# Attention's first tiles, image 0's convolution and gates, and the gathering of results: four edits in a transformer kernel

## The chip, the cores and the metric

The kernel runs on one core of a Trainium2 chip, whose engines TensorE (PE), VectorE (DVE), ScalarE (ACT) and GpSimd (POOL) run their own instruction streams, while SyncE (SP), ACT and POOL issue transfers (DMA). The metric is the device time of one execution in microseconds, as the median of several runs. Everything is float32.

## The reference

The input x is 4 images of 384 channels and 32 x 32 pixels (1024 tokens each, 4096 in all).

```python
# layer 0
x = x + conv0(_ln_c(x))      # attention: 8 heads of 48, q k and v by one matrix of 384 x 1152
#   attn = q k^T + q table_k[idx] + (k table_q[idx])^T, softmax, out = attn v + (attn summed by idx) table_v, projection
#   idx: the clipped offset (dy, dx) of two pixels, 15 x 15 of them
t = t + ffn0(_ln_t(t))       # factored (Kronecker) weights, gelu
# layer 1
x = x + conv1(_ln_c(x))      # depthwise: 7x7 + 5x3 + 3x5 + (1x7, 7x1) + (1x5, 5x1) + bias
probs = softmax(_ln_t(t) @ gate_w + gate_b)   # 4 experts, the best 2, weights made to sum to 1
t = t + sum over the 2 experts of weight * (gelu(_ln_t(t) @ w1[e] + b1[e]) @ w2[e] + b2[e])
```

## The kernel before

The work is in three phases, one after the other.

`qkv_phase` (to 233 us) takes 8 tiles t of 512 tokens, two to an image. For each, PE makes six 128 x 512 blocks of q and k, DVE scales each into `qk_sb` (four buffers) and POOL's queue stores it to `qk_d` in DRAM (L168); the next tile's statistics follow; then PE makes v in four blocks of 128 tokens, which ACT scales into `va`, a tile that holds v of all heads and tokens. After every second tile `va`'s part of one image (2 MB) is stored to `v_d` on POOL's queue (L183). After tiles 2 to 5, POOL's queue also writes zeros over a quarter of `xs_d` (L191), in two writes of 3 MB each; `xs_d` will hold the rows of tokens sorted by expert.

`attention_phase` (233 to 1681 us) takes the heads in turn, some 176 us each. For a head, `load_tables` brings the table `tab` and the head's q or k (`kq`) in and `load_keys` the keys as the scores use them (`kk`); PE multiplies tables and q or k (`tabq_ps`, `tabk_ps`), DVE transposes 32-wide blocks (L306), ACT copies to `st`, and SP stores to `sd` in DRAM, from where the position terms come back in the order of the scores. Then for each of 32 rows of pixels: the bias is summed on POOL (L352), scores on PE, their sum and maximum on DVE (L380), exponentials on ACT (L390), transposes and products with v. The next head's loads and table products run in the shadow of the present head's; those of the first head have nothing to hide behind. Its loads stand on ACT's queue. The memory of this phase lies over that of the qkv phase, so that `kq`, `kk`, the memory of `arow` and that of `den` wait for the last read of `va`. Matmuls and loads of this phase are kept in the order in which they are written (`pin`); most others are ordered by a scheduler that estimates costs, so that the built order on an engine need not be that of the code.

`rest_phase` (from 1681 us) begins with `enter(0)`, that is `front(0)` (attention's projection, its residual, and the first feed-forward), and with `first()` (normalisation and convolution of image 0). The convolution's 49 taps are split by channel chunk k and rows: `convolve` runs on DVE, one multiply-add per tap and part (L996), and `taps_by_matmul` on PE, with a diagonal weight block per tap; sums of even and odd taps stand in two halves of two banks (`tap_ps`), are folded by a further matmul into a bank `taps_ps` (L1050), which is single, and DVE adds that to `xb` (L1053). Of image 0, DVE has chunk 0 and half of chunk 1, PE chunk 2 and the other half of chunk 1. `dispatch(0)` then makes the gates (`gates`: logits, token statistics, weights and mask) and sorts the tokens: positions, and 16 indirect writes (`scatter`). All that concerns images 1 to 3 is one generator, `others()`, called `todo`: `front`, normalisation, convolution on DVE, gates and scatter of each image, cut in steps. Two of its steps are run per step of `dispatch(0)`.

Then come 67 blocks of 128 sorted tokens (`blocks`), about 16 us each: POOL gathers a block's rows (`xg`) and, when the expert changes, weights (`w`), PE transposes the rows and makes both products (L1193, L1175), and steps of `todo` are mixed in while their estimated DVE time is behind that of PE. In the last group of blocks, after the sixth, `combine(range(B - 1))` is mixed in too, one step per half block: for every 256 tokens of images 0 to 2, four indirect gathers of expert outputs `y`, a weighted sum (ACT, then DVE at L1243), six transposes on PE (`out_ps`, L1221), an addition to the residual `xr` (a load from `x2_d`, one buffer), and the output store on SP's queue. `combine([3])` follows after the last block.

Of the kernel before, what the change touches and what calls it, by code (L numbers as in the profile page):

```python
# [11 lines left out]
F32 = mybir.dt.float32  # L12
AF = mybir.ActivationFunctionType
# [5 lines left out]
P = 128  # L19
# [16 lines left out]
VW = 64  # L36
# [84 lines left out]
def qkv_phase(tc, cst, x, w_qkv, qk_d, v_d, xs_d):  # L121
# [6 lines left out]
    with ExitStack() as es:  # L128
# [22 lines left out]
        for t in range(NT // TOK):  # L151
            b, n0 = divmod(t * TOK, N)
            xt = xts.pop(t)
            _, rstd = stats
            ps = to_partitions(nc, (work, psum, "st"), ident, one, rstd)
            scale = work.tile([P, TOK], F32, tag="scale", name="scale")
            nc.scalar.copy(scale, ps)
            if t + 1 < NT // TOK:
                load(t + 1)
            for m in range(2 * KC):  # L160
                ps = psmm.tile([P, TOK], F32, tag="mm", name="qk_ps")
                for k in range(KC):
                    nc.tensor.matmul(
                        ps, wq[:, k, m * P : (m + 1) * P], xt[:, k, :], start=(k == 0), stop=(k == KC - 1)
                    )
                sb = ev.tile([P, TOK], F32, tag="qk", name="qk_sb")
                nc.vector.tensor_tensor(sb, ps, scale, ALU.mult)
                nc.gpsimd.dma_start(qk_d[m * P : (m + 1) * P, t * TOK : (t + 1) * TOK], sb)  # L168
            if t + 1 < NT // TOK:
                stats = result(token_stats(nc, (work, psum, "st"), ident, xts[t + 1], cst["eps6"]))  # L170
            for j in range(TOK // P):
                ps = psmm.tile([P, TOK], F32, tag="mm", name="v_ps")
                for k in range(KC):
                    nc.tensor.matmul(
                        ps[:, :C], xt[:, k, j * P : (j + 1) * P], wq[:, k, 2 * C :], start=(k == 0), stop=(k == KC - 1)
                    )
                nc.scalar.activation(
                    va[:, :, t * (TOK // P) + j, :HD], ps[:, :C].rearrange("p (h d) -> p h d", d=HD),
                    AF.Copy, scale=rstd[:, j, :],
                )  # L180
            if n0 + TOK == N:
                w = NBLK * VW
                nc.gpsimd.dma_start(  # L183
                    v_d.rearrange("h p n -> p h n")[:, :, b * w : (b + 1) * w],
                    va[:, :, b * NBLK : (b + 1) * NBLK, :].rearrange("p h c d -> p h (c d)"),
                )
            if 2 <= t < 2 + NEXP:
                rows = xs_d[(t - 2) * CAP : (t - 1) * CAP].rearrange("(n p) c -> p n c", p=P)
                n = rows.shape[1] // 2
                for r in (rows[:, :n], rows[:, n:]):  # L190
                    nc.gpsimd.dma_start(r, bcast(zero, 1, r.shape[1]))  # L191


def attention_phase(tc, cst, tabs, tv, qk_d, v_d, ao_d, heads):

# [28 lines left out]
    with ExitStack() as es:  # L226
# [24 lines left out]
            den.append(d)  # L251


        kq = fixed.tile([64 + HD, NT], F32, name="kq")
        kk = fixed.tile([64 + HD, B, N // 2], F32, name="kk")
        tab = fixed.tile([64 + HD, SPAN, ZW], F32, name="tab")
        vb = fixed.tile([P, B, NBLK, VW], F32, name="vb")
        aT = fixed.tile([P, NBLK, YB, P], F32, name="aT")
        a1t = fixed.tile([P, 4, IMG, YT, B], F32, name="a1t")
        tvw = fixed.tile([P, 4, IMG, HD], F32, name="tvw")  # L260

        def load_tables(h):
            for lo, i, r0 in ((64, 0, h * HD), (0, 1, C + h * HD)):
                bulk(tab[lo : lo + HD], tabs[i, h])
                yield
                for b in range(B):
                    bulk(kq[lo : lo + HD, b * N : (b + 1) * N], qk_d[r0 : r0 + HD, b * N : (b + 1) * N])
                    yield
# [239 lines left out]
            sd = dram.tile([P, IMG, SPAN * IMG], F32, tag="sd", name="sd")  # L508
            return [{"h": h, "y": y, "sd": sd} for y in range(IMG)], prepare(h, sd)

        for _ in load_tables(heads[0]):
            pass
        load_keys(heads[0])
        blk, tables = new_head(heads[0])
# [323 lines left out]
def rest_phase(tc, cst, x, ao_d, ins, xs_d, y_d, x2_d, out):  # L838
# [9 lines left out]
    with ExitStack() as es:  # L848
# [167 lines left out]
        def taps_by_matmul(xb, parts):  # L1016
# [10 lines left out]

            half = small.tile([P, 64], F32, tag="half", name="half", bufs=1)
            nc.vector.tensor_tensor(half, ident[:, :64], ident[:, 64:], ALU.add)
            diag = {k: diagonals(k, w) for k, w in zip(dict.fromkeys(k for k, _ in parts), wts[1])}  # L1030
            yield
            for k, y0 in parts:
                sums = [ps_y.tile([P, TOK], F32, tag="y", name="tap_ps", bufs=2) for _ in range(2)]
                for t0 in range(0, 49, 2):
                    for t in range(t0, min(t0 + 2, 49)):
                        dy, dx = divmod(t, 7)
                        for h in range(2):
                            lo = 64 * h
                            nc.tensor.matmul(
                                sums[h][64 * (t % 2) : 64 * (t % 2) + 64].rearrange("p (y x) -> p y x", x=IMG),  # L1040
                                diag[k][lo : lo + 64, t, :],
                                img[lo : lo + 64, k, dy + y0 : dy + y0 + TOK // IMG, dx : dx + IMG],
                                start=(t < 2), stop=(t > 46),
                            )
                    yield
                po = ps_y.tile([P, TOK], F32, tag="t", name="taps_ps")
                for h in range(2):
                    e = hid.tile([P, TOK], F32, tag="hs", name="taps", bufs=HS)
                    nc.scalar.copy(e, sums[h])
                    nc.tensor.matmul(po[64 * h : 64 * h + 64], half, e, start=True, stop=True)  # L1050
                yield
                acc = xb[:, k, y0 * IMG : y0 * IMG + TOK]
                nc.vector.tensor_tensor(acc, acc, po, ALU.add)  # L1053
                yield

        def new(shape, name, dt=F32):
# [151 lines left out]
        def combine(bs):  # L1208
# [13 lines left out]
                    nc.vector.tensor_tensor(xr[:, c0:c1, :], xr[:, c0:c1, :], ps[:, : c1 - c0, :], ALU.add)  # L1222
                nc.sync.dma_start(out[b, :, n0 : n0 + w].rearrange("(k p) n -> p k n", p=P), xr)

            late = None
            for b, n0 in ((b, n0) for b in bs for n0 in range(0, N, w)):
                t0 = b * N + n0
                if n0 == 0 and not end:
                    result_rows(nc, small, images[b], pieces)
                    if b + 2 == B:  # L1230
                        result_rows(nc, small, images[b + 1], pieces)
                    yield 3.0, 0.0
                zs = []
                for j in range(2):
                    ys = []
                    for s in range(2):
                        y = new_row() if end else ld.tile([P, C], F32, tag=f"yt{s}", name=f"yt{s}")
                        index = images[b]["pos"][:, n0 // P + j, s : s + 1]
                        nc.gpsimd.indirect_dma_start(y, None, y_rows, bass.IndirectOffsetOnAxis(ap=index, axis=0))
                        ys.append(y)  # L1240
                    gate = images[b]["gate"][:, n0 // P + j, :]
                    nc.scalar.activation(ys[0], ys[0], AF.Copy, scale=gate[:, 0:1])
                    nc.vector.scalar_tensor_tensor(ys[0], ys[1], gate[:, 1:2], ys[0], ALU.mult, ALU.add)  # L1243
                    zs.append(ys[0])
                if end:
                    if late:
                        finish(*late)
                    xr = xbs[b][:, :, n0 : n0 + w]
                    late = (b, n0, xr, zs)
                    yield 0.0, 0.0  # L1250
                else:
                    xr = ld.tile([P, KC, w], F32, tag="xr", name="xr", bufs=1)
                    nc.sync.dma_start(xr, x2_d[:, t0 : t0 + w].rearrange("(k p) n -> p k n", p=P))
                    for _ in range(6):
                        yield 0.4, 0.1
                    finish(b, n0, xr, zs)
            if late:
                finish(*late)

        xbs = {}  # L1260

# [8 lines left out]
        def first():  # L1270


            taps = taps_by_matmul(xbs[0], [(2, 0), (2, IMG // 2), (1, IMG // 2)])
            next(taps)
            halves = []
            yield from normalise(xbs[0], halves)
            yield from image(halves)
            for _ in convolve(0, xbs[0], [(0, 0, IMG), (1, 0, IMG // 2)]):
                for _ in range(2):
                    next(taps, None)  # L1280
                yield
            for _ in taps:
                pass
            preload(wts[1])
# [40 lines left out]
        for i, _ in enumerate(first()):  # L1325
            if 6 <= i < 8:
                next(todo)
        for _ in dispatch(0):
            for _ in range(2):
                next(todo)  # L1330
        clock = [0.0, 0.0]

# [28 lines left out]
def metaformer_kernel(ctx: ExitStack, tc: tile.TileContext, ins, out):  # L1361
# [15 lines left out]
    x2_d = dram.tile([C, NT], F32, name="x2_d")  # L1377
    xs_d = dram.tile([NEXP * CAP, C], F32, name="xs_d")
    y_d = dram.tile([ALL * BLK, C], F32, name="y_d")
    qkv_phase(tc, cst, ins["x"], ins["w_qkv"], qk_d, v_d, xs_d)  # L1380
    attention_phase(tc, cst, ins["tabs"], ins["tv"], qk_d, v_d, ao_d, list(range(HEADS)))
    rest_phase(tc, cst, ins["x"], ao_d, ins, xs_d, y_d, x2_d, out)


# [66 lines left out]
```

## Time and profile before

| | us |
|---|---|
| median of 3 runs | 3321.61 (3317.27 to 3322.02) |
| the profiled execution | 3319.24 |
| its span | 3317.4 |
| PE busy | 2985.4 (90%) |
| DVE busy | 2012.0 (61%) |
| ACT busy | 1327.9 (40%) |
| POOL busy | 1149.2 (35%) |

All busy times are within the span; what is outside the span (1.8 us) is the start and end of the execution that no instruction covers. A profile row of a group gives line, engine, operation, output and input with their shapes, the number of instructions, busy time and the mean of one in ns. A row of waits gives the engine and what it was about to run, then the instruction or transfer that released it, total us, times and longest. In rows of stretches, the number in brackets counts instructions, and after the five engines come the granted PE clock (1.00 is full), the busy share of the DMA engines and GB/s. Lines are those of the kernel before.

### The profile page before, as it was taken

What the parts mean: (1) busy time and instruction counts of PE and PEld (TensorE: products, weight loads), DVE (VectorE), ACT (ScalarE), POOL (GpSimd) and SP (SyncE); (2) the same over time, 40 slices, a digit from 0 to 9 for tenths busy, and PEclk for the clock granted to TensorE, in tenths of its full rate; (3) what the DMA queues carried; (4) which work ended last, traced back from release to release, by engine and by line L of the source; (5) the groups of instructions that cost most, each with busy time, mean ns of one, the idle gap of its engine ahead of it and who ended that gap; (6) DMA issues with size and microseconds to landing.
All of it is one profiled execution on the core that took longest, in us unless ns stands there. A gap on an engine that the chain in (4) does not pass through costs nothing.

```text
span 3317.4 us, 63687 instructions
## 1 busy us (share of the span) xinstructions
PE 2985.4 (90%) x25391; PEld 2067.9 (62%) x25391; DVE 2012.0 (61%) x3618; ACT 1327.9 (40%) x2682; POOL 1149.2 (35%) x1096
## 2 busy tenths in 40 slices
PE   8988898989898989898879697999999999999897
PEld 4445666656675666666643354576677777777675
DVE  2226777867677777777748779999999520002101
ACT  1115555555555655565511131443342423333222
POOL 3113636363636364544520031123124231214312
PEclk9998999999999999999989888999999999999898
DMA  8637464555455554646240222271344044466652
GB/s 308 242 115 208 111 183 118 171 132 163 127 173 127 160 147 132 178 120 189 69 151 25 100 69 100 83 289 55 119 184 184 27 179 156 155 262 220 230 203 72
DMA packets 222136, 500.57 MB, mean 151 GB/s; under 512 B 92128, under 2 KB 144992, under 8 KB 214160
## 3 DMA queue, kind: packets, MB, share of 16 engines
q1 hardware_dynamic: 156080, 212.81, 21.0%
q0 software_dynamic: 43488, 228.24, 18.7%
q10 hardware_dynamic: 22272, 55.46, 6.8%
q8 instruction: 200, 3.28, 0.4%
q14 instruction: 96, 0.79, 0.1%
HBM read 543.58 MB, written 152.37 MB: 210 GB/s over the span
## 4 chain that ended last, share of the span: by engine, by line
PE 61%; DVE 12%; issue 9%; DMA 7%; ACT 6%; POOL 4%; SPq 1%; ACTq 0%; POOLq 0%; DVEq 0%
PE e_ps L1193 13%; PE y_ps L1175 13%; DVE xb L996 7%; PE av_ps L216 6%; PE tabq_ps L216 5%; PE t_ps L409 5%; PE sc_ps L216 4%; PE tv_ps L216 3%; ACT arow L390 2%; PE tabk_ps L216 2%; ACT aT L410 2%; PE a_ps L419 2%; DMA qs<-qk_d 2%; DVE oT L473 2%; POOL bias L352 1%
## 5 line engine op out<-in xcount | busy, mean ns | idle before, releaser
L352 POOL TENSOR_TENSOR bias<-b,s 128x416 f32<-128x416 f32 (+24 forms) x656 | 659.5, 1042 | 654.6 <-DMA s<-sd 474.3
L1193 PEld LDWEIGHTS e_ps<-xT,w 128*128 128x128 f32 x4824 | 660.0, 194 | 238.4 <-issue 17.0
L1193 PE MATMUL e_ps<-xT,w 128*128 128x128 f32 x4824 | 680.0, 279 | 23.4 <-DVE xb L909 9.2
L1175 PE MATMUL y_ps<-w,eh 128*128 128x384 f32 x1608 | 656.0, 493 | 8.7 <-DVE yo L1178 4.8
L996 DVE SCALAR_TENSOR_TENSOR xb<-img,c_w,xb 128x1024 f32<-128x1024 f32 (+1 forms) x539 | 630.2, 1227 | 0.0
L1196 ACT ACTIVATE eh<-e_ps,w 128x128 f32<-128x128 f32 x804 | 294.4, 368 | 765.0 <-PE e_ps L1193 750.7
L380 DVE CUSTOM_DVE_ANT_0 arow<-sc_ps,bias 128x1024 f32<-128x1024 f32 x256 | 312.6, 1221 | 192.3 <-POOL bias L352 80.3
L1165 POOL DMA_INDIRECT w<-in_w,row x134 | 163.9, 1223 | 747.6 <-PE y_ps L1175 232.3
L401 DVE TENSOR_REDUCE extra<-arow 128x32 f32<-128x32 f32 (+24 forms) x768 | 378.8, 551 | 28.3 <-ACT arow L390 28.0
L409 PEld LDWEIGHTS t_ps<-ident,arow 128*128 128x128 f32 x2048 | 227.6, 144 | 265.5 <-ACT arow L390 184.0
L410 ACT COPY aT<-t_ps 128x512 f32<-128x512 f32 x512 | 276.0, 589 | 266.0 <-PE t_ps L409 249.9
L390 ACT ACTIVATE arow<-arow,nm 128x1024 f32<-128x1024 f32 x256 | 297.1, 1161 | 177.9 <-DVE nm L380 166.8
L409 PE MATMUL t_ps<-ident,arow 128*128 128x128 f32 x2048 | 290.0, 286 | 77.4 <-ACT arow L390 74.5
L1178 DVE TENSOR_TENSOR yo<-y_ps,w 128x384 f32<-128x384 f32 x67 | 37.1, 553 | 496.0 <-PE y_ps L1175 496.0
L216 PE MATMUL sc_ps<-kk,qs 48*32 48x512 f32 x4096 | 295.8, 623 | 46.6 <-DVE nm L380 27.6
L1175 PEld LDWEIGHTS y_ps<-w,eh 128*128 128x128 f32 x1608 | 250.2, 194 | 22.2 <-ACT eh L1196 5.2
L306 DVE STREAM_TRANSPOSE b<-tabk_ps 128x480 f32<-128x480 f32 x256 | 219.7, 979 | 62.2 <-PE tabq_ps L216 36.8
L216 PEld LDWEIGHTS av_ps<-aT,vb 128*64 128x64 f32 x4096 | 223.0, 137 | 52.8 <-ACT aT L410 38.0
L216 PE MATMUL tabq_ps<-tab,kq 48*128 48x480 f32 x512 | 225.2, 587 | 19.9 <-DMA kq<-qk_d 19.9
L216 PE MATMUL av_ps<-aT,vb 128*64 128x128 f32 x4096 | 238.4, 275 | 0.3 <-ACT aT L410 0.3
L216 PE MATMUL tabk_ps<-tab,kq 48*128 48x480 f32 x512 | 225.4, 587 | 0.0
L216 PEld LDWEIGHTS tabq_ps<-tab,kq 48*128 48x128 f32 x512 | 147.6, 296 | 57.7 <-issue 26.5
(217 smaller groups left out, 3147.1 us busy)
## 6 DMA issues: line engine op xcount, KB each, us to landing
sd<-st SPq DMA_DIRECT2D x128, 480.0 KB, 2.5
s<-sd SPq DMA_DIRECT2D x512, 120.0 KB, 3.3
xs_d<-zero POOLq DMA_DIRECT2D x8, 3072.0 KB, 11.4
tvw<-in_tv ACTq DMA_DIRECT2D x120, 192.0 KB, 3.7
y_d<-yo SPq DMA_DIRECT2D x67, 192.0 KB, 2.0
qk_d<-qk_sb POOLq DMA_DIRECT2D x48, 256.0 KB, 3.4
qs<-qk_d SPq DMA_DIRECT2D x256, 48.0 KB, 2.9
kq<-qk_d ACTq DMA_DIRECT2D x64, 192.0 KB, 3.7
```

The source lines that it names most:

```text
L216: ins = nc.tensor.matmul(*args, **kw)
L306: turn = nc.vector.transpose(b2.rearrange("p e y x -> p x (e y)")[:, i + j], ps[:, j, : SPAN * IMG])
L352: nc.gpsimd.tensor_tensor(bias[:, y0:y1, :], bass.AP(b2.tensor, b2.offset + (e * IMG + y0) * IMG, [list(b2.ap[0]), [(step * IMG + 1) * IMG ...
L380: nc.vector.tensor_tensor_reduce(s["flat"], ps.rearrange("p h n -> p (h n)"), s["bias"].rearrange("p y x -> p (y x)"), -SCALE, BIG, ALU.ad ...
L390: nc.scalar.activation(s["flat"], s["flat"], AF.Exp, bias=s["nm"], scale=-1.0, accum_out=dn[:, y % YT : y % YT + 1])
L401: pin(nc.vector.tensor_reduce(ex[:, i, :], a[:, p0:p1, :].rearrange("p y x -> p x y"), AX.X, ALU.add))
L409: pin(nc.tensor.transpose(pt[:, j, :], s["flat"][:, k0 : k0 + P], ident))
L410: pin(nc.scalar.copy(aT[:, 4 * g : 4 * g + 4, s["y"] % YB, :], pt))
L996: nc.vector.scalar_tensor_tensor(acc[:, k, y0:y1], img[:, k, dy + y0 : dy + y1, dx : dx + IMG], w7[:, k, dy, dx : dx + 1], acc[:, k, y0:y1 ...
L1175: nc.tensor.matmul(py, hs, w[:, o : o + C], start=(ff == 0), stop=(ff == NF - 1))
L1193: nc.tensor.matmul(ph, w[:, o : o + P], xT[k][:, c, :], start=(c == 0), stop=(c == KC - 1))
L1196: nc.scalar.activation(hs, ph, AF.Gelu, bias=w[:, o : o + 1])
```

## The change

Four things change.

- `kq`, `kk` and `tab` come from a pool `held` that is opened before the qkv phase, so that they have memory of their own. The first head's tables are loaded on SP's queue instead of ACT's. v is stored to `v_d` after every tile (1 MB), and the zero writes are kept in program order, where the scheduler had placed them singly before.
- In image 0's convolution, DVE has chunk 0 and 4 rows of chunk 1; PE has chunk 2 in two parts of 16 rows and the other 28 rows of chunk 1 in two parts of 14. The steps of PE's taps are taken three instead of two per tap of DVE.
- `dispatch(0)` takes no step of `todo` in its first six steps, and three per step after that.
- In the combine, the gathers and the residual load of a chunk of 256 tokens are issued one chunk ahead; the rows stand in the 16 buffers named `rows`, the residual has two buffers; a chunk has ten steps instead of six. All images' result rows are made first. At the end all 16 gathers are issued ahead of the sums.

```diff
-            if n0 + TOK == N:
-                w = NBLK * VW
-                nc.gpsimd.dma_start(
-                    v_d.rearrange("h p n -> p h n")[:, :, b * w : (b + 1) * w],
-                    va[:, :, b * NBLK : (b + 1) * NBLK, :].rearrange("p h c d -> p h (c d)"),
-                )
+            w = NBLK // 2 * VW
+            nc.gpsimd.dma_start(
+                v_d.rearrange("h p n -> p h n")[:, :, t * w : (t + 1) * w],
+                va[:, :, t * NBLK // 2 : (t + 1) * NBLK // 2, :].rearrange("p h c d -> p h (c d)"),
+            )
...
-                    nc.gpsimd.dma_start(r, bcast(zero, 1, r.shape[1]))
+                    tc.keep_in_program_order(nc.gpsimd.dma_start(r, bcast(zero, 1, r.shape[1])))
...
-        kq = fixed.tile([64 + HD, NT], F32, name="kq")
-        kk = fixed.tile([64 + HD, B, N // 2], F32, name="kk")
-        tab = fixed.tile([64 + HD, SPAN, ZW], F32, name="tab")
+        kq, kk, tab = held
...
-        for _ in load_tables(heads[0]):
+        for _ in load_tables(heads[0], dma):
             pass
...
-            for k, y0 in parts:
+            for k, y0, ny in parts:
+                n = ny * IMG
...
-            late = None
-            for b, n0 in ((b, n0) for b in bs for n0 in range(0, N, w)):
-                ...
-                        y = new_row() if end else ld.tile([P, C], F32, tag=f"yt{s}", name=f"yt{s}")
-                ...
-                    xr = ld.tile([P, KC, w], F32, tag="xr", name="xr", bufs=1)
-                    nc.sync.dma_start(xr, x2_d[:, t0 : t0 + w].rearrange("(k p) n -> p k n", p=P))
-                    for _ in range(6):
-                        yield 0.4, 0.1
-                    finish(b, n0, xr, zs)
+            def results(b, n0):
+                zs = []
+                for j in range(2):
+                    ys = [new_row() for _ in range(2)]
+                    for i, y in enumerate(ys):
+                        index = images[b]["pos"][:, n0 // P + j, i : i + 1]
+                        nc.gpsimd.indirect_dma_start(y, None, y_rows, bass.IndirectOffsetOnAxis(ap=index, axis=0))
+                    zs.append(ys)
+                if end:
+                    return zs, xbs[b][:, :, n0 : n0 + w]
+                t0 = b * N + n0
+                xr = ld.tile([P, KC, w], F32, tag="xr", name="xr")
+                nc.sync.dma_start(xr, x2_d[:, t0 : t0 + w].rearrange("(k p) n -> p k n", p=P))
+                return zs, xr
+
+            def weigh(b, n0, zs):
+                ...
+            if not end:
+                for b in (*bs, B - 1):
+                    result_rows(nc, small, images[b], pieces)
+                    yield 3.0, 0.0
+            todo = [(b, n0) for b in bs for n0 in range(0, N, w)]
+            ahead = {}
+            for i, (b, n0) in enumerate(todo):
+                for more in todo[i : i + (len(todo) if end else 2)]:
+                    if more not in ahead:
+                        ahead[more] = results(*more)
+                zs, xr = ahead[b, n0]
+                for _ in range(0 if end else 5):
+                    yield 0.3, 0.0
+                zs = weigh(b, n0, zs)
+                for _ in range(0 if end else 5):
+                    yield 0.3, 0.1
+                finish(b, n0, xr, zs)
...
-            taps = taps_by_matmul(xbs[0], [(2, 0), (2, IMG // 2), (1, IMG // 2)])
+            half, own = IMG // 2, 4
+            rest = (IMG - own) // 2
+            taps = taps_by_matmul(
+                xbs[0], [(2, 0, half), (2, half, half), (1, own, rest), (1, own + rest, rest)]
+            )
...
-            for _ in convolve(0, xbs[0], [(0, 0, IMG), (1, 0, IMG // 2)]):
-                for _ in range(2):
+            for _ in convolve(0, xbs[0], [(0, 0, IMG), (1, 0, own)]):
+                for _ in range(3):
                     next(taps, None)
                 yield
...
-        for _ in dispatch(0):
-            for _ in range(2):
+        for i, _ in enumerate(dispatch(0)):
+            for _ in range(3 if i > 5 else 0):
                 next(todo)
...
+    with tc.tile_pool(name="held", bufs=1) as pool:
+        held = [
+            pool.tile([64 + HD, *n], F32, name=name)
+            for name, n in (("kq", [NT]), ("kk", [B, N // 2]), ("tab", [SPAN, ZW]))
+        ]
+        qkv_phase(tc, cst, ins["x"], ins["w_qkv"], qk_d, v_d, xs_d)
+        attention_phase(tc, cst, held, ins["tabs"], ins["tv"], qk_d, v_d, ao_d, list(range(HEADS)))
```

## The prediction

> **What bounds the kernel now.** I read the page first: shares of the engines, then the chain that ended last.
>
> ```profile
> span 3317.4 us, 63687 instructions
> ...
> PE 2985.4 (90%) x25391; PEld 2067.9 (62%) x25391; DVE 2012.0 (61%) x3618; ACT 1327.9 (40%) x2682; POOL 1149.2 (35%) x1096
> ...
> PE 61%; DVE 12%; issue 9%; DMA 7%; ACT 6%; POOL 4%; SPq 1%; ACTq 0%; POOLq 0%; DVEq 0%
> ```
>
> PE is the bound almost everywhere, so a gain can only come out of the 332 us in which it is idle, or out of work that it does at half clock. Where those are is read from busy times by stretch (start:end in us, length, busy us of each engine with its instruction count, granted PE clock, DMA share, GB/s). I cut the span where the stages that the change touches begin and end:
>
> ```profile
> 90.00:105.00 15.00, 10.44 (x34) 5.90 (x33) 4.56 (x12) 1.46 (x3) 2.28 (x3) 0.89 1.02 386
> 233.00:294.00 61.00, 36.73 (x160) 25.45 (x160) 27.33 (x35) 19.67 (x34) 7.85 (x10) 0.77 0.77 227
> 1778.00:1876.00 98.00, 75.61 (x605) 32.20 (x598) 93.06 (x102) 4.47 (x8) 0.00 (x0) 0.88 0.20 77
> 1876.00:1959.00 83.00, 71.90 (x266) 30.97 (x267) 47.51 (x170) 32.10 (x59) 24.94 (x23) 0.90 0.23 80
> 2600.00:2985.00 385.00, 380.13 (x2302) 298.89 (x2301) 42.67 (x238) 125.77 (x320) 85.27 (x85) 0.99 0.45 166
> 2985.00:3135.00 150.00, 127.50 (x750) 101.01 (x750) 30.26 (x55) 45.61 (x112) 65.31 (x67) 0.92 0.64 211
> ```
>
> Each is a place where PE is short of work or slow: 4.6 us idle with DMA saturated; 24 us at attention's start; 22 us in image 0's convolution, where DVE is full; 22.5 us in the combine against 5 in the 385 us before it. The chain over attention's start (start, length, what) and one step of it at 80 us:
>
> ```profile
> 80.14 16.01 DMA qk_d<-qk_sb
> ...
> 234.29 7.51 DMA v_d<-va
> 242.57 2.00 ACTq L224
> 246.01 6.39 DMA kq<-qk_d
> 252.86 5.94 PE tabq_ps L216 x7
> 262.77 0.39 PE tabq_ps L216
> 284.37 2.52 DMA sd<-st
> 291.80 1.88 POOL bias L352
> ```
>
> The last qkv matmul ends at 232.96; the 2 MB store of v must be read out of `va` before anything of attention may overwrite that memory; then the tables and q load; PE starts at 252.86, at half clock. Last, VectorE's forms in the convolution (mean ns of one), and what PE waited for there and in 2985 to 3135 (total, times, longest):
>
> ```profile
> L996 DVE SCALAR_TENSOR_TENSOR xb<-img,c_w,xb 128x1024 f32<-128x1024 f32 x49 | 62.4, 1274 | 0.0
> L996 DVE SCALAR_TENSOR_TENSOR xb<-img,c_w,xb 128x512 f32<-128x512 f32 x49 | 36.3, 740 | 0.0
> ```
> ```profile
> PE taps_ps L1050 <- DVE xb L1053: 18.8, 1, 18.8
> ```
> ```profile
> PE out_ps L1221 <- DVE yt L1243: 16.6, 5, 10.1
> PE xT_ps L1159 <- DMA xg<-xs_d,slot: 5.7, 2, 3.7
> ```
>
> **Attention's start.** `kq`, `kk` and `tab` no longer share addresses with `va`, and their first loads stand on SP's queue, in the built order among the qkv tiles; the last is issued with the last tile, about 4 us ahead of PE's end. So PE's first table product waits only for its own queue: from the end E of the qkv matmuls, about E+0.6, against 19.9 us before, and the clock doesn't fall. What still waits for the last v store (now one tile, 1 MB; the 2 MB took 7.51 us, so about 4 with issue and semaphore to E+6) are the memsets of `arow` and `den`, and behind `den` on DVE the 31 table transposes: 261.28 to 288.75 before, 25.9 us of work (0.81 us each), so E+6.5 to E+32.5. The last `st` copy stood 4.4 us ahead of their end, and the first bias on POOL 6.8 us behind that copy (store, reads, q loads): E+28 to E+31, bias at E+35 to E+38. Before it was 291.2 − 233.0 = 58.2. I take 37: **−21**, bounds −23 and −19. SP takes these ten loads and the first two of q; it had nothing but x tiles and weights there.
>
> **The qkv stage itself.** Before, one tile (t=2) took 31.8 us where the others take 25.36; its first evacuation waited for a `qk_d` store that took 16.01 us, queued on POOL behind a 3 MB zero write and the 2 MB v store. That loss, 6.5, can go. Against it: the eight zero writes, spread before over 15 to 106 us, are now two together behind the v store of t = 2 to 5. A tile then moves x 0.79, q and k 1.57, v 1.05, zeros 6.29 and about 0.39 MB of early q loads: 10.1 MB. If only POOL's queue counts (a zero write drains in 7.6 to 9 us, so 17 for a pair, 2.8 for v, 2 for the x tile it meets, and latencies: 25.7 us), a tile is 0.3 us over PE's 25.36: 1.4 in four. The Trainium skill (*DMA: Bandwidth & Descriptors*, "Issuing engines are not separate DMA queues") says that queues of all issuers end on the same 16 engines and interleave, so that moving loads to SP buys no bandwidth; with the 386 GB/s of the saturated row, 10.1 MB take 26.2 us: 0.8 a tile, 3.3 in four. The row at 1.02 DMA share agrees that the engines, not a queue, are full; I take 3.3. Net **−3**, bounds −6.5 and +6. PE's v part isn't behind the late evacuations (in the built order DVE's two last ones follow the next tile's statistics), which is why a late store costs no more than its own overrun.
>
> **Image 0's convolution.** DVE's second form shrinks from 512 to 128 elements. Start to start a pair takes 1.858 us (1.196 and 0.662), which gives 1.043 ns an element and 0.128 fixed: 0.26 us. 49 × (1.196 + 0.26) = 71.4 against 91.0: DVE's taps end at 1849.7 rather than 1869.8. PE takes 4 more rows in a fourth part. 98 matmuls of 512 columns took 22.02 us, of 448: 19.3, twice, instead of 22.02 once. Without a wait: 1774.4 + 23.8 + 22.0 + 2 × 19.3 + three joints of 1.9 = 1864.5, and gates would end about 8 us earlier than before. But in the built order the sums' second bank `taps_ps` is single, the add that frees it for part 3 stands on DVE behind all 98 taps, and part 4 stands on PE behind part 3's fold. So PE, through part 3 at 1843.5, waits to about 1851: 1851 + 1.9 + 19.3 = 1872.2, and starts part 4 cold. For that the Trainium skill (*TensorE: Matmul & The Clock Gate*, "The HAM clock gate") gives about 3.4 us of half speed after an idle window, 1.7 us lost; the trace had table products at 0.80 us rather than 0.39 from 252.86 to 262.77, 9.9 us, that is 4.9 lost. That was after a 20 us wait, this is 7; I take 2, nearer the page, up to 4.9 in the range. Then fold and add, 2.6, and the 12 gate matmuls at full clock, 2.8 (4.64 at half before): gates at 1879.5 against 1874.5: **+5**, not the −20 that DVE's saving suggests; bounds −8 (if the taps' order on PE gives way) and +8.
>
> **Gates undivided.** Before, front(1) ran on PE between the steps of gates and positions, and PE was busy for 71.9 of the 83 us to the first expert block at 1955.4. Now the gates run first, and front(1) three steps at a time behind: the scatter (16 × 1.275 us on POOL, from 1924.2) comes some 26 us earlier and is covered by PE's work. The first block still stands behind front(1) and the normalisation of image 1 on PE, since it is moved, not removed: 1879.5 + 72 = 1951.5 to 1952. What can go is the 11 us of idle: −8 against where the gates end, **−3** with the +5 above; bounds −8 and +6. DVE starts image 1's taps by the same amount earlier and is full till 2597, so the shift is kept.
>
> **The combine.** PE is idle for 22.5 of 150 us and at clock 0.92 instead of 0.99, which is another 9 on 127.5 busy; at the rate of the row before (1.3%) 2 us would stay: at most 28 to gain. The causes are a weighted row late for the output transposes (16.6 us, with a residual load that had one buffer and stood behind an output store), and block rows late behind POOL's gathers (5.7). The change issues the four gathers of a chunk one chunk ahead, in 16 shared buffers, and gives the residual load two: the 16.6 us and their cold clock go. Not the gathers: 48 of 1.26 us remain on POOL, in bursts of four (5 us) between weight and block loads, and a burst makes a block's rows late as before. 28 minus 5 to 10 of that: **−18**, bounds −28 and −8. At the very end 16 gathers of 1.26 us bound the tail in both: 0.
>
> **Sum.** −21 − 3 − 3 − 18 = −45 against the profiled 3319.24 us (span 3317.4 and 1.8 around it): 3274. That run was 2.4 below the median of the runs shown, 3321.6, so against the median: **3277**.
>
> **Rivals.**
> Convolution does gain: if the taps on PE don't wait for DVE, gates end about 8 earlier rather than 5 later, the stall of t=2 goes whole and the combine runs like the stretch before it: −24 − 6 − 16 − 28 = −74, 3248. For it: DVE at 93 of 98 us is the bound there. Against: the single bank.
> Only the start gains: zeros cost what t=2 lost, the gates' shift is eaten by the later start, and y gathers still delay block rows: −21 + 3 from the start, −4 from the combine: −22, 3300. For it: POOL is 65 of 150 us busy there, already the fullest in any stretch after 2600.
> Slower: paired zeros stop the qkv stage. If PE has to wait until the whole pair has drained, each of four tiles loses up to those 17 us. The other parts give −42 and the stall of t=2 another −6.5, so from 12 us a tile on it takes all; at 17 it is 68 − 48.5 = +19.5: 3341. For it: the 16.01 us landing behind a single zero write and v. Against it: `qk_sb` has four buffers, and 5 MB ahead of a store cost one stall of 6.5.
> It doesn't do what it says: that is the convolution's forecast above, part of the sum.
>
> **How the numbers follow.** Forecast 62 in 100 (its own range 3262 to 3294), convolution too 12, start only 20, slower 5, within 0.2% (6.6 us, about what a measurement of this kernel can tell from no change) 1. The likeliest is 3277. The bounds of the parts rarely fall together; 3254 to 3305 leaves out most of the second case's lower half and all of the slower one, under 2 in 10. Faster 0.94, same 0.01, slower 0.05.
>
> **What would show it.** First table product within 2 us of the last v matmul and at full clock; first bias 35 to 38 us behind that. All eight tiles between 25 and 27 us, none at 31. DVE's taps 71 to 73 us long, and PE waiting there some 7 us for an add, gates ending some 101 us behind the first tap, 96 before. PE's wait for the weighted rows gone, that for block rows larger. Wrong it would be if tiles 3 to 6 take over 30 us, or if PE stays idle over 15 us in the combine.

## The result, and the profile after

The changed kernel takes 3289.95 us (median of 4 runs, 3283.6 to 3295.78), the kernel before 3321.82 us beside it (4 runs, 3317.27 to 3323.29): a ratio of 0.9906, 95% interval 0.9885 to 0.9927. The forecast was 3277, with 3254 to 3305 around it. So 32 us went where 45 were forecast; the parts are further from their forecasts than the sum is.

The page of the changed kernel:

```profile
span 3289.7 us, 64044 instructions
...
PE 2980.7 (91%) x25591; PEld 2065.0 (63%) x25591; DVE 1992.4 (61%) x3619; ACT 1332.1 (40%) x2687; POOL 1146.6 (35%) x1100
...
PE 46%; DVE 10%; issue 6%; ACT 4%; DMA 3%; POOL 1%; SPq 0%; ACTq 0%; POOLq 0%; DVEq 0%
```

The span is 27.7 us shorter and PE's busy time 4.7: 23 us of the gain are idle time of PE. (The chain of this trace covers only 70% of the span and does not reach attention's start, so I read that stage from waits and timelines.) The stretches of the changed kernel, cut where its own stages begin and end (columns as before):

```profile
237.40:279.50 42.10, 36.29 (x161) 22.21 (x160) 27.52 (x34) 19.64 (x34) 5.08 (x8) 0.92 0.65 245
...
1767.30:1868.40 101.10, 90.42 (x783) 39.76 (x776) 74.00 (x103) 4.18 (x8) 0.00 (x0) 0.95 0.13 49
1868.40:1933.20 64.80, 61.17 (x255) 26.81 (x256) 35.46 (x154) 33.09 (x58) 25.11 (x25) 1.00 0.41 140
1933.20:2049.80 116.60, 80.38 (x367) 55.18 (x366) 111.09 (x137) 21.58 (x48) 11.50 (x7) 0.81 0.13 44
...
2984.60:3105.60 121.00, 117.62 (x728) 93.43 (x728) 21.92 (x40) 41.91 (x106) 58.37 (x59) 1.00 0.66 230
```

From the last v matmul to the first bias it is 42 us instead of 58. From the first tap on VectorE to the end of the gates' matmuls it is 101 instead of 96. From there to the first expert block PE is idle for 3.6 us instead of 11. In the combine it is idle for 3.4 us at full clock. But the stretch from the first expert block to the third block's output has become worse: 117 us with PE idle for 36. For these two stretches the kernel before had

```profile
1874.50:1955.40 80.90, 69.81 (x257) 28.08 (x255) 43.91 (x166) 31.26 (x59) 22.83 (x23) 0.92 0.24 85
1955.40:2054.60 99.20, 76.65 (x357) 54.55 (x358) 96.18 (x115) 19.91 (x46) 15.78 (x10) 0.83 0.14 48
```

so the second was 99 us with 22.5 idle. Following a few marks through both traces (starts and ends of instructions, us; "block n" is the output of the n-th expert block, counted from 0) shows where the gain is made and lost:

| mark | before | changed, difference |
|---|---|---|
| last v matmul ends | 233.0 | +4.4 |
| first bias | 291.2 | −11.7 |
| first projection | 1687.8 | −10.2 |
| VectorE's last tap of image 0 starts | 1869.7 | −30.6 |
| image 0's gate matmuls end | 1874.5 | −6.1 |
| first expert matmul | 1955.4 | −22.2 |
| first tap of image 1 | 1958.6 | −12.0 |
| last tap of image 3 | 2597.6 | −8.3 |
| block 27 | 2597.2 | −4.2 |
| block 50 | 2986.2 | −1.6 |
| block 57 | 3137.4 | −31.7 |
| block 66, the last | 3285.4 | −27.9 |
| end | 3317.4 | −27.7 |

All that three of the four parts won in 2000 us is nearly gone at block 50; the combine then brings 26. (Between blocks 30 and 37 every other trace loses 2.4 to 3.3 us against this one trace of before, whatever was edited: that belongs to this execution of before, not to the change. Without it the changed kernel would stand at about −4 at block 50.) Marks of single traces scatter: kernels that have the changed start and the same code up to the first projection stand there at −10.2 to −15.5, so 2 or 3 us between two traces prove little by themselves.

### The profile page after: what moved, and what is told of

Read it like the earlier page. It is cut to its first block, busy times and chain, and to the rows that moved or that the text cites. A ratio compares the mean times of both kernels' runs of the same rounds, so it can differ in the third digit from the quotient of the medians.

```text
span 3289.7 us, 64044 instructions
## 1 busy us (share of the span) xinstructions
PE 2980.7 (91%) x25591; PEld 2065.0 (63%) x25591; DVE 1992.4 (61%) x3619; ACT 1332.1 (40%) x2687; POOL 1146.6 (35%) x1100
## 4 chain that ended last, share of the span: by engine, by line
PE 46%; DVE 10%; issue 6%; ACT 4%; DMA 3%; POOL 1%; SPq 0%; ACTq 0%; POOLq 0%; DVEq 0%
PE e_ps L1191 14%; PE y_ps L1173 13%; DVE xb L993 6%; PE av_ps L215 3%; PE t_ps L406 3%; PE tabq_ps L215 2%; PE sc_ps L215 2%; PE tv_ps L215 1%; ACT arow L387 1%; PE a_ps L416 1%; ACT aT L407 1%; PE proj_ps L903 1%; DVE oT L470 1%; PE row_ps L75 1%; PE tabk_ps L215 1%
## 5 line engine op out<-in xcount | busy, mean ns | idle before, releaser
L1173 PE MATMUL y_ps<-w,eh 128*128 128x384 f32 x1608 | 654.9, 493 | 21.7 <-DVE yo L1176 13.7
L993 DVE SCALAR_TENSOR_TENSOR xb<-img,c_w,xb 128x1024 f32<-128x1024 f32 (+1 forms) x539 | 610.9, 1192 | 0.0
L215 PE MATMUL sc_ps<-kk,qs 48*32 48x512 f32 x4096 | 292.1, 625 | 54.0 <-DMA qs<-qk_d 27.7
L215 PE MATMUL tabk_ps<-tab,kq 48*128 48x480 f32 x512 | 226.1, 588 | 2.9 <-DVE b L303 2.9
L308 ACT COPY st<-tabq_ps 128x480 f32<-128x480 f32 x256 | 141.6, 560 | 76.0 <-PE tabk_ps L215 38.6
```

What stands on the lines that cost most here:

```text
L215: ins = nc.tensor.matmul(*args, **kw)
L993: nc.vector.scalar_tensor_tensor(acc[:, k, y0:y1], img[:, k, dy + y0 : dy + y1, dx : dx + IMG], w7[:, k, dy, dx : dx + 1], acc[:, k, y0:y1 ...
L1173: nc.tensor.matmul(py, hs, w[:, o : o + C], start=(ff == 0), stop=(ff == NF - 1))
```

## The experiments

### Each part alone

Each takes one of the change's four parts into the kernel before; the diffs are those parts of the diff above.

> The kernel before with the first part of the change alone (held tiles, tables on SP's queue, v stored per tile, zero writes kept in program order). Theory: the shift made at attention's start is kept by everything behind it, since nothing else is altered: last v matmul at 237 (233 before), first bias at 279 to 280 (291.2), first projection about 10 us earlier, end 8 to 12 us earlier. Rival: what is won ahead of the stretch in which VectorE is the bound (1955 to 2597) is given back there, whatever won it; then the first projection is 10 us earlier but the end only 0 to 4.

> The kernel before with image 0's convolution cut anew, alone. Theory: VectorE's taps end 20 us earlier, TensorE waits some 9 us for an add and runs its fourth part cold; the gates end 4 us later than before, the end is 3 to 6 us later. Rival: the four us are covered in the stretch in which VectorE is the bound, since VectorE came free earlier: end within 2 us of before.

> The kernel before with image 0's gates undivided, alone. Theory: first expert block 14 to 18 us earlier, image 1's taps on VectorE 4 to 8 us earlier, but TensorE then waits longer for VectorE in the first blocks, and the blocks behind the VectorE stretch are not earlier: end between 2 us earlier and 6 us later. Rival: taps and blocks keep the 6 us: end 5 to 8 us earlier.

> The kernel before with the combine's gathers issued 256 tokens ahead, alone. Theory: nothing moves up to 2985, then TensorE's waits for weighted rows go and the last group is 24 to 28 us shorter; end 24 to 28 us earlier. Rival (as forecast): gathers in bursts delay block rows; 18 us or less.

| part alone | ratio to before (95%) | first projection | gates end | first tap of image 1 | block 50 | end of the span |
|---|---|---|---|---|---|---|
| attention's start | 0.9966 (0.9954 to 0.9979) | −13.5 | −13.4 | −13.4 | −10.2 | −12.2 |
| convolution | 1.0000 (0.9985 to 1.0015) | −1.8 | +2.6 | +1.2 | +3.5 | +4.1 |
| gates | 0.9986 (0.9975 to 0.9996) | −0.2 | −0.1 | −6.1 | +2.0 | 0.0 |
| combine | 0.9925 (0.9897 to 0.9953) | +1.2 | +1.4 | +1.4 | +6.5 | −19.5 |

The marks are differences to the one trace of before, as above. The start keeps what it wins all the way: its rival, that the stretch bound by VectorE swallows whatever is won ahead of it, falls. The convolution alone costs 4.4 us up to the gates (−1.8 to +2.6), by the wait that the forecast named, seen in this kernel's waits of PE:

```profile
PE taps_ps L1051 <- DVE xb L1054: 8.9, 1, 8.9
```

In the timed runs that loss is not told from nothing. The combine is worth 26 from block 50 on (+6.5 to −19.5), as in the changed kernel, and 25 in the timed runs. Its own edits (gathers a chunk ahead, two buffers for the residual, ten steps, the result rows first) were not tried apart. The gates alone bring the first expert matmul 16 us and image 1's taps 6 us forward, and PE's waits in the first blocks (1930 to 2060) grow from 9.2 and 4.8 to

```profile
PE e_ps L1193 <- DVE xb L909: 14.5, 1, 14.5
PE y_ps L1175 <- DVE yo L1178: 13.7, 1, 13.7
```

The trace ends where before ended; the timed runs say 4.6 us less (1.3 to 8.3), so alone the gates may be worth a few us. Whether the two parts in the middle are worth their place was tried without them:

> The kernel before with the first part (attention's start) and the last (combine) alone, without the new cut of the convolution and the undivided gates. Theory, from the traces of single parts: convolution and gates together give nothing at the end, so this is as fast as the changed kernel or up to 5 us faster, 3281 to 3292. Rival, from the timed runs of single parts: the gates give 4 to 5 us, so this is 4 us slower, 3292 to 3298.

The ratio is 0.9891 (0.9867 to 0.9915), 3282.26 us against 3315.65 beside it; the changed kernel's is 0.9906. The first theory holds: convolution and gates as they stand give nothing that the runs can show. The trace of start_combine even ends 8.5 us ahead of the changed kernel's, but 5.3 of these stood already at the first projection, ahead of both parts.

### What holds the qkv stage

One edit to the changed kernel, the zero writes no longer kept in order:

```diff
-                    tc.keep_in_program_order(nc.gpsimd.dma_start(r, bcast(zero, 1, r.shape[1])))
+                    nc.gpsimd.dma_start(r, bcast(zero, 1, r.shape[1]))
```

> The changed kernel with one thing undone: the zero writes are not kept in program order, so that the scheduler places them singly early on (in the built order one to three per tile, the last behind the fifth v store at the latest). Theory: it is the two writes behind one another that make TensorE wait for free q and k buffers, 31.7, 27.2 and 26.3 us in tiles 5 to 7; without them all tiles take 25.4 to 27 and the last v matmul ends at 227 to 230 instead of 237.4, and the whole is 8 to 10 us shorter. Rival: the early loads on SP's queue and v stores of single tiles fill the transfer engines; then a tile among the early ones takes 31 as before, the last v matmul ends at 233 to 236, 2 to 4 us are won.

3283.5 us, ratio 0.9898 (0.9879 to 0.9917). Lengths of the tiles, from the end of one tile's last v matmul to that of the next (us; t = 1 to 7), and where the last one ends:

| kernel | t = 1 | 2 | 3 | 4 | 5 | 6 | 7 | last v |
|---|---|---|---|---|---|---|---|---|
| before | 25.4 | 31.8 | 25.4 | 25.4 | 25.4 | 25.4 | 24.1 | 233.0 |
| changed | 25.4 | 25.4 | 25.4 | 26.0 | 31.7 | 27.2 | 26.3 | 237.4 |
| attention's start alone | 25.4 | 25.4 | 25.4 | 25.7 | 32.5 | 26.3 | 25.8 | 236.8 |
| zeros spread | 29.6 | 26.9 | 27.0 | 25.4 | 25.4 | 25.4 | 24.1 | 233.3 |
| zeros taken out | 25.4 | 25.4 | 25.4 | 25.4 | 25.4 | 25.4 | 24.1 | 226.1 |

So the theory falls: the pairing costs only 4 of the 11 us, the loss moves to the early tiles. How the pairs make PE wait can be read from the changed kernel's waits (PE from 0 to 240, POOL from 100 to 245):

```profile
PE qk_ps L163 <- DVE qk_sb L167: 8.2, 4, 4.3
POOL xs_d L190 <- issue: 52.3, 4, 14.7
```

POOL stands for 11.8 to 14.7 us ahead of the second zero write of each pair, and the q and k stores that are written behind it are issued only then. VectorE waits for one of its four `qk_sb` buffers (up to 14.5 us, for a store to land), and PE for VectorE. In zeros_spread PE has no such wait; it waits 5.0 us for statistics that VectorE makes behind evacuations which are late in the same way.

Either the loads and v stores or the 25 MB of zeros as such had to be the cause. The next kernel takes the zeros out of the stage, and tries the convolution's order too. That order had been tried alone first: the adds of PE's sums kept among VectorE's taps.

```diff
-                nc.vector.tensor_tensor(acc, acc, po[:, :n], ALU.add)
+                tc.keep_in_program_order(nc.vector.tensor_tensor(acc, acc, po[:, :n], ALU.add))
...
-                        nc.vector.scalar_tensor_tensor(
+                        tap = nc.vector.scalar_tensor_tensor(
...
+                        if not b:
+                            tc.keep_in_program_order(tap)
...
-            for _ in convolve(0, xbs[0], [(0, 0, IMG), (1, 0, own)]):
-                for _ in range(3):
-                    next(taps, None)
+            taken = 0
+            for t, _ in enumerate(convolve(0, xbs[0], [(0, 0, IMG), (1, 0, own)])):
+                while taken < 27 * (t + 1) / 15.5:
+                    next(taps, None)
+                    taken += 1
```

> The changed kernel with VectorE's adds of TensorE's sums put in order among its taps (behind the 15th, 31st and 46th of 49) instead of behind all of them. Theory: TensorE's 9 us wait and the 2 us of its cold fourth part go, the gates of image 0 end 10 to 12 us earlier than in the changed kernel, and so does the first expert block; but of that TensorE loses part again waiting for VectorE in the first blocks, since VectorE starts image 1's taps by less; end 4 to 11 us earlier. Rival: VectorE then waits for TensorE between its taps and the gates end no earlier than 3 us before those of the changed kernel; end within 3 us.

3271.26 us, ratio 0.9863 (0.9845 to 0.9882). In this kernel image 0's residual is stored ahead of the last of the four adds, so that sum is missing from what it computes; its work up to the gates isn't touched by that. PE's wait for the add is gone. The stretch from VectorE's first tap to the end of the gates takes 90.3 us instead of 101.1 (96.4 before), and the first tap of image 1 comes 11.6 earlier than in the changed kernel; at the end it is 15, some 2 of which stood already at the first projection. The theory holds, though the loss that it expected behind the gates did not come. Then, with the store behind the last add:

```diff
-            if 2 <= t < 2 + NEXP:
-                ...
-                    tc.keep_in_program_order(nc.gpsimd.dma_start(r, bcast(zero, 1, r.shape[1])))
...
+        zero = wp.tile([P, 1, C], F32, name="zero")
+        nc.vector.tensor_scalar(zero[:, 0, :], xbs[0][:, KC - 1, N - C :], 0.0, None, ALU.mult)
+        for e in range(2 * NEXP):
+            rows = xs_d[e * CAP // 2 : (e + 1) * CAP // 2].rearrange("(n p) c -> p n c", p=P)
+            nc.gpsimd.dma_start(rows, bcast(zero, 1, rows.shape[1]))
         preload(wts[0])
```

> The changed kernel with two edits: VectorE's adds of the sums among its taps (as tried before, here with the residual's store behind the last add), and the zero writes taken out of the qkv stage and issued after image 0's first feed-forward, where the transfer engines are at 0.2 to 0.4. Theory: the 25 MB of zeros are what the qkv stage cannot carry beside its own transfers, wherever they stand in it (8 us lost with pairs, 7.9 with single ones); without them all tiles take 25.4 and the last v matmul ends at 226 to 228; the adds give 10 to 15 more. End 20 to 27 us earlier than in the changed kernel, 3263 to 3270. Rival: early loads and v stores cost the stage as much; then the last v matmul still ends at 231 or later, and only the adds' 10 to 15 are seen.

3262.33 us, ratio 0.983 (0.9805 to 0.9856), the fastest complete version here, 0.8% below the changed kernel by the two ratios. All tiles are at 25.4 (the last at 24.1) and the last v matmul ends at 226.1: without the zeros beside them, early loads and single v stores cost the stage nothing. Against 226.1 the zeros cost 6.9 before, 11.3 in the changed kernel and 7.2 spread (the expectation's 8 and 7.9 were other counts); other traces with the stage of before have 5.6 to 6.4, other traces with pairs 9.8 to 10.7. Where they stand now there is room for them: from 1752 to 1850 the transfer engines come to a share of 0.71 and PE works on at full clock, its third and fourth part at 19.30 us each with no wait for VectorE:

```profile
1752.00:1850.00 98.00, 95.45 (x819) 45.37 (x812) 78.93 (x123) 10.85 (x22) 6.94 (x6) 1.00 0.71 275
```
```profile
1796.20 19.30 PE L1033 MATMUL tap_ps<-img,w 64*64 64x448 f32 x196
...
1817.50 19.30 PE L1033 MATMUL tap_ps<-img,w 64*64 64x448 f32 x196
```

(The first line is a stretch, the others the timeline of PE: start, length, instructions.)

### What the undivided gates are worth

```diff
-        for i, _ in enumerate(dispatch(0)):
-            for _ in range(3 if i > 5 else 0):
+        for _ in dispatch(0):
+            for _ in range(2):
                 next(todo)
```

> As zeros_late, but with image 0's gates mixed with image 1's steps as before the change (two per step). Theory: with gates undivided VectorE starts image 1's taps 6 us earlier, but TensorE loses 7 to 14 us waiting for VectorE in the first blocks; so this is within 3 us of zeros_late. Rival: the undivided gates are worth their 6 us, and this is 4 to 8 us slower.

3263.03 us, ratio 0.9827 (0.9802 to 0.9851): the same. Its first expert matmul is 19 us later than in zeros_late and image 1's first tap 7 us; at block 4 it is 4.5 behind, at block 12 it is 1.9 ahead, and the spans end 0.2 apart. It was 2.8 us behind already at the first projection, ahead of the edit, so undivided gates win nothing here and may cost 2 or 3 us. The wait of PE for VectorE's `yo` is 1.8 us in it and 13.7 in zeros_late.

### What the table transposes wait for

The last v store lands 7.7 us after its issue in the changed kernel, and VectorE's memset of `den`, with the transposes behind it, starts then (the issues from 236 to 250: KB each, us to landing; and VectorE's timeline, with idle time before):

```profile
sd<-st SPq DMA_DIRECT2D x4, 480.0 KB, 5.7
v_d<-va POOLq DMA_DIRECT2D x1, 1024.0 KB, 7.7
kk<-qk_d ACTq DMA_DIRECT2D x2, 384.0 KB, 6.5
```
```profile
246.71 0.13 DVE L249 MEMSET den<- 128x32 f32 x2 [16.32 <-DMA sd<-st]
246.76 3.48 DVE L303 STREAM_TRANSPOSE b<-tabk_ps 128x480 f32<-128x480 f32 x4
```

The row names the table's store `sd` as what came last; the v store lands at the same time. First I moved `va` to addresses that `b2` and `den` don't share:

```diff
-        va = wp.tile([P, HEADS, B * NBLK, VW], F32, name="va")
+        va = vp.tile([P, HEADS, B * NBLK, VW], F32, name="va")
+        gap = wp.tile([P, 3584], F32, name="gap")
...
+            d = pool.tile([P, IMG], F32, name=f"den{i}")
```

> The changed kernel with the memory of va moved off that of the tables b2 and of den, so that nothing on VectorE waits for the last store of v (7.7 us after the last v matmul here). Theory: that wait is what stands between the last v matmul and the table transposes; they start 1 to 3 us after it instead of 9.3, and the first bias comes 35 to 37 us after it instead of 42.1: 5 to 7 us for the whole. Rival: the transposes then run at the pace of table products and transfers, the first bias comes 40 us or more after it, 2 us or less.

3287.76 us, ratio 0.9914 (0.9894 to 0.9934), and the transposes start 9.9 us behind the last v matmul. This didn't test the theory: in the built kernel the first transpose waits for fifteen semaphores, and that of the last v store is still among them. Why it is there was not found out; a wait set for the memory of the whole stage would do it. So the store itself was left out, from zeros_late:

```diff
-            nc.gpsimd.dma_start(
-                v_d.rearrange("h p n -> p h n")[:, :, t * w : (t + 1) * w],
-                va[:, :, t * NBLK // 2 : (t + 1) * NBLK // 2, :].rearrange("p h c d -> p h (c d)"),
-            )
+            for u in {6: (6, 7), 7: ()}.get(t, (t,)):
+                nc.gpsimd.dma_start(
+                    v_d.rearrange("h p n -> p h n")[:, :, u * w : (u + 1) * w],
+                    va[:, :, u * NBLK // 2 : (u + 1) * NBLK // 2, :].rearrange("p h c d -> p h (c d)"),
+                )
```

> As zeros_late, with the v store of the last tile left out: its part of v_d is filled a tile earlier with the zeros that va then holds, so v of the last 512 tokens is missing from the result. Theory: that store is what holds the table transposes, since every memory of attention waits for it; without it they start 2 to 4 us behind the last v matmul instead of 9, and the first bias comes 34 to 36 us behind it instead of 40 to 42, so 5 to 7 us less in all. Rival: the transposes wait for something else that ends at that time (store of the first table products, loads); then 2 us or less.

3257.12 us, ratio 0.981 (0.9783 to 0.9837). VectorE's timeline in it:

```profile
226.34 0.13 DVE L243 MEMSET den<- 128x32 f32 x2 [7.70 <-ACT va L175]
230.82 4.28 DVE L297 STREAM_TRANSPOSE b<-tabk_ps 128x480 f32<-128x480 f32 x5 [4.35 <-PE tabq_ps L209]
```

The memset comes 0.7 us behind the last v matmul (225.7) instead of 9.6 in zeros_late, so it was the v store. But the transposes then wait 4.35 us more for the first table products, in whose order `tabk_ps` stands behind seven `tabq_ps`; they start at 5.2 and the first bias comes at 35.8 instead of 40.9. The wait for the store is worth 5.1 us in these two traces, and no more, since the next thing is late by half of it. (In the eight traces that have the changed start and this wait, the first bias comes 39.6 to 42.7 us behind the last v matmul, so 35.8 is clear of them; the timed runs of the two kernels, 5 us apart, overlap.)

## Why the prediction was right, and where not

The range held the time and the sign was right, in part by luck: the combine brought 8 us more than forecast and the gates 10 less. Step by step, the differences from the two profiled traces:

| step of the sum | forecast | measured |
|---|---|---|
| qkv stage | −3 (−6.5 to +6) | +4.4 |
| attention's start | −21 (−23 to −19) | −16.1 |
| convolution, to the gates' end | +5 (−8 to +8) | +4.1 |
| gates, kept to the last blocks | −8 | −16 at the first block, −6 at image 1's taps, about +2 at block 27, so nothing kept |
| combine | −18 (−28 to −8) | −26.3 |

The rest of the −27.7 lies where nothing was forecast: +1.5 over attention, +2.6 from block 27 to 50 and +0.2 in the tail. Of the signs that were named, the first table product at full clock, the length of VectorE's taps (72.2 us) and the 101 us to the gates' end came true; the first bias did not (42 us, not 35 to 38), nor did tiles of 25 to 27 us: t = 5 took 31.7, over the 30 that were named as a sign of being wrong. PE's idle time in the combine stayed far under the 15 us named there.

**The qkv stage.** The direction of the loss was seen, its size was not. The tiles behind the pairs lost 0.7, 6.3, 1.8 and 2.2, 11.0 together, where 3.3 were taken. Of the two readings that were weighed there, 3.3 by the rule of the Trainium skill (*DMA: Bandwidth & Descriptors*, "Issuing engines are not separate DMA queues", by which queues of all issuers share the same engines) was nearer than the single queue's 1.4, but that does not show it to be the right one. The loads on SP, for which I took it, cost nothing without the zeros, as zeros_late shows. If the rate is what sets the loss, the mis-sized term is that rate: 11.0 over four tiles of 25.4 makes 28.1 us a tile, and 10.1 MB in that time are 359 GB/s, not the 386 of the row that I took; from 150 to 222 us the profile has 331 GB/s at a share of 0.92, with two gaps. But 22.86 of the 23.86 MB moved in these 72 us came through POOL's own queue, in whose order the q and k stores stand behind the zeros, POOL stood 52 us ahead of the second writes, and undoing the pairs alone was worth 4 us in zeros_spread. The forecast's count of that queue took 17 us for a pair to drain; here the second write alone was issued 13 to 16 us behind the first. Rate and order are not told apart by these runs: zeros on another queue within the stage would do it, and were not tried.

**Attention's start.** PE starts 0.67 us behind the last v matmul at full clock, as forecast. The step "so about 4 with issue and semaphore to E+6" failed: half the bytes of v took the same time, 7.7 us against 7.51. A store of 1 MB with nothing on the other queues took 5.1 (in zeros_late_mixed, issued at 177.7), so some 2.6 are owed to the 0.79 MB of keys and the first table stores that now run beside it, and 4 was too little in any case. VectorE started at E+9.3, not E+6.5. And the 32 transposes took 29.7 us from the first start to the last end, not 26: the forecast took their busy time, where the trace of before has 27.5 from start to end, and now PE, which had run ahead of VectorE, stood for 2.92 us and then made table products at half clock (0.80 us apart instead of 0.40) until 255. The clock that was to be saved was lost a second time.

```profile
248.63 1.17 PE L215 MATMUL tabk_ps<-tab,kq 48*128 48x480 f32 x1 [2.92 <-DVE b L303]
```

**The convolution.** Right in mechanism and size. The wait for the add was 8.99 us (7 to 8 forecast), the fourth part took 21.44 us instead of 19.30:

```profile
1840.20 1.76 PE L1048 MATMUL taps_ps<-taps,half 128*64 128x448 f32 x4 [8.99 <-DVE xb L1051]
1841.89 21.44 PE L1037 MATMUL tap_ps<-img,w 64*64 64x448 f32 x196
```

So the slow clock cost 2.1, near what was taken from the Trainium skill's page *TensorE: Matmul & The Clock Gate* ("The HAM clock gate"; about 1.7) and not the 4.9 of the trace's row. With the adds among the taps both go, and the stretch is 10.8 us shorter.

**The gates.** "DVE starts image 1's taps by the same amount earlier and is full till 2597, so the shift is kept" is the step that failed. VectorE's taps did stay ahead (−12.0 to −8.3). But PE has hardly more room there: from block 2 to block 27 it is busy for 522 of 543 us in the trace of before, VectorE for 536. What counts at the end is PE's time, and its idle part was moved: 7.5 us fewer before the first block (11.1 to 3.6; the other half of the 16 is work at full clock, 61.2 us instead of 69.8 at 0.92), 13.7 more in the first blocks (22.5 to 36.2), where its outputs and projections wait for a VectorE that is full of taps. At block 2 all of it is gone (−4.8, with −6.1 at the gates). In the changed kernel:

```profile
PE y_ps L1173 <- DVE yo L1176: 13.7, 1, 13.7
PE e_ps L1191 <- DVE xb L906: 13.6, 1, 13.6
```

**The combine.** The bound of 28 was nearly reached (its own terms, 22.5 and 9 less 2, give 29.5). "and a burst makes a block's rows late as before" is what failed: in 2985 to 3106 PE waits for no gathered row at all, and for weighted rows once:

```profile
PE e_ps L1191 <- ACT xT L1158: 1.7, 3, 0.6
PE out_ps L1219 <- DVE rows L1243: 1.5, 1, 1.5
```

So the bursts of four gathers on POOL delay nothing that PE needs: the 5.7 us for block rows went too, and nothing had to be taken off the 28 for them. Why the block rows were late three times before and no longer are was not taken apart.

**The rivals.** "Only the start gains" was right that the gates' shift is eaten, but its sum up to the combine was −18, against −1.6 at block 50, and its −4 for the combine was −26. "Slower" would have needed 12 us a tile; the worst tile lost 6.3. "The convolution does gain" needed its adds in another order, and with that order it does.

## What to carry to other kernels

Where one engine is busy for 96% of a stage, as PE is here from block 2 to 27, work that is brought to it earlier is a gain only if less of its time is idle or slow in all: look at what it will wait for next, before counting the shift as kept. Background transfers belong in a stretch where the transfer engines have room: in the qkv stage the zeros cost 11 us in pairs and still 7 when spread, and at most 1 behind the first feed-forward (from the first projection to the gates' end 181.8 us in zeros_late, 181.2 in conv_adds). And a cut of work between two engines is only as good as the order on the engine that frees the buffers: from the first tap to the gates' end the same cut took 101 us with its adds behind the taps and 90 with them between, where the old cut took 96.

## What was not expected of the hardware

A store of 1 MB took 7.7 us from issue to landing, as long as one of 2 MB that ran alone (7.51); with nothing on the other queues one of 1 MB took 5.1. What else is moving counted for as much as the size.

With the wait for it removed, only 5.1 of its 9 us came back. And zero writes of 25 MB made a stage 7 to 11 us longer at a mean transfer share that left room on paper (0.65 over the stage of the changed kernel, but 0.92 from 150 to 222).
